# Moving the loads and stores of the normalised inputs, and the inputs of the output stage, from SyncE's DMA queue to those of ScalarE and GpSimd

## The chip, the cores and the metric

The kernel runs on one core of a Trainium2 chip. The time is the device time of one execution in microseconds, as the median of several runs; the profile is that of one further execution. Engines are called as in the profile: PE (TensorE), DVE (VectorE), ACT (ScalarE), POOL (GpSimd) and SP (SyncE). SP computes nothing here; it issues DMAs. ACT and POOL can issue DMAs too, each on a queue of its own and in the order of its own instructions.

## The reference

One layer over 8 sequences of 256 tokens with 512 features, all in float32:

```
xn = layernorm(x)
q, k, v = xn @ wq.T, xn @ wk.T, xn @ wv.T      # 32 query heads, 8 key and value heads, 128 wide
q, k = rotary(q), rotary(k)
scores = q k^T / sqrt(128), rescaled for some keys, causal
s = softmax(scores) v @ wo.T
gates = softmax over the two best of 4 experts of xn @ router_w.T
delta = sum over experts of gate * (xn @ A_e.T) @ B_e.T * 4
out = x + s * silu(delta)
```

## The kernel before

The 2048 tokens go through in four blocks (`tb`, 0 to 3) of two sequences (`b`, 0 and 1). For every block the kernel loops over the 8 groups of key heads (`g`). One step of a group makes the queries of the next group, computes scores and softmax for this one, multiplies the transposed probabilities with the values of the one before, and adds a part of the output projection. All large products use a scheme of seven block products in place of eight (the tiles `S1`, `S2`, `S4` and the operations `w`, `s`, `acc` that add tiles up). PSUM tiles that the profile names: `paq`, `peq`, `pdq` (queries), `pak`, `pek`, `pdk` (keys), `sc` (scores), `av` (values), `po` (output).

*Order.* No engine's order is written by hand. Every piece of work is a job in a `Plan`, given by `add(engine, takes, what, after, opens, closes, near, lag)`: the engine that it runs on, how long it occupies it, the jobs before it, the buffers that it takes and frees, a hint when it is due, and `lag`, the time from its end until its result can be used (a DMA's landing). The order of PE's jobs is laid by hand as due times. `Plan.run` plays the jobs through on the host with these costs and a hop of 0.18 us between engines; on each engine it starts the job that is due first among those that are ready. The instructions of an engine are issued in the order that comes out, and on the chip each waits for what it really depends on. All of them are recorded by a helper, so the profile gives line 118 for nearly everything.

*Normalised inputs.* `norm(tb)` loads the four row tiles `x` of a block, computes mean and deviation on DVE, and makes `xn`. The products need `xn` with features on partitions, the tile `XB`. For the first block PE transposes it. For the other three this is done with DVE and DMAs. DVE transposes 32x32 blocks (`turn_blocks`, profile name `x<-xn`); `spread(b)` stores the result to DRAM in four DMAs (`turned<-x`, 128 KB each); `gather(b)` reads it back in four DMAs (`XB<-turned`, 128 KB each, in pieces of 32 floats). DVE then adds up four tiles `XT` from both halves `b` of `XB`. There is one `XB` buffer (the room `X`), so a block's first gather waits until PE has read the last block's `XB` for the last time. In the plan, `gather(1)` also waits for the landing of `gather(0)`.

*Probabilities.* In `softmax(tb, g, b)`, ACT takes exponentials into `p`, DVE scales them and transposes 32x32 blocks into `blocks`. SP then stores these in four DMAs (`there<-blocks`) and, when they have landed, loads the transposed tile in one DMA of 768 KB (`pT<-there`), from which PE computes `av`. ACT copies `av` to `a`. There is one `p` and one `blocks` buffer.

*Output of a block.* `put_together(tb)` adds the seven accumulated products up. Its `inputs(b)` loads the gates (`g<-gates`) and rows of x (`xf<-in_x_dram`), 512 KB each, for the blocks 0 to 2; DVE multiplies and adds them, and SP stores the result. The last block has a function of its own, `last_products`.

*Queues.* Before the change SP issues the loads of `x`, both bounces (`turned`/`XB` and `there`/`pT`), the stores of the gates, `g` and `xf`, and the results. POOL issues the weight loads (`w`, `wo`, from rings of nine and eight tiles) and the stores of weight sums. ACT issues two table loads at the start and no other DMA.

Of the kernel before, what the change touches and what calls it, by code (L numbers as in the profile page):

```python
# [169 lines left out]
class Plan:  # L170
# [10 lines left out]
    def add(self, engine, takes, what, after=(), opens=(), closes=(), near=None, lag=0.0):  # L181
        after = [a for a in after if a]
        job = Job(engine, takes, what, after, opens, closes, near, lag, len(self.jobs))
        for a in after:
            a.then.append(job)
        for hold in closes:
            hold.readers += 1
        self.jobs.append(job)
        return job
# [71 lines left out]
def layer(ctx: ExitStack, tc: tile.TileContext, x, wquad, woquad, raT, bT, table, out):  # L261
    nc = InOrder(tc)
    pool = lambda name, bufs, **kw: ctx.enter_context(tc.tile_pool(name=name, bufs=bufs, **kw))
# [32 lines left out]
    add = plan.add  # L296
    rooms = {}

    def hold(tag):
        return Hold(rooms[tag])  # L300
# [9 lines left out]
    gates, sums_of, acts, weights, x_hold, loaded = {}, {}, {}, {}, {}, {}  # L310
# [7 lines left out]
    def norm(tb):  # L318
# [4 lines left out]
        xs, box = {}, {}  # L323
        xh = [hold("x") for _ in range(NB)]
# [42 lines left out]
        def new_acts():  # L367
            acts[tb] = (
                one.tile([P, NB, 2, 2, S], F32, tag="XB", name=f"XB{tb}"),
                one.tile([P, 4, 2, S], F32, tag="XT", name=f"XT{tb}"),  # L370
            )
# [6 lines left out]
        def turn_blocks(t):  # L378

            to = xs["x", t // 2].rearrange("p t d -> p (t d)")  # L380
            nc.vector.transpose(
                to.rearrange("p (q k t s) -> p t k q s", q=NQ, k=DC, t=2)[:, t % 2],
                box[t].rearrange("p (k q s) -> p k q s", q=NQ, s=BLK),
            )

        def spread(b):
            there = box["there", b] = turned.tile(
                [NQ, BLK, NQ, 2 * P], F32, tag=f"turned{b}", name=f"turned{tb}_{b}"
            )
            for a in range(NQ):  # L390
                nc.sync.dma_start(
                    out=there[:, :, a, :].rearrange("q r e -> r q e"),
                    in_=xs["x", b][bass.ts(a, BLK)]
                    .rearrange("r t d -> r (t d)").rearrange("r (q e) -> r q e", q=NQ),
                )

        def gather(b):
            if b == 0:
                new_acts()
            to = acts[tb][0][:, b].rearrange("p h c (t a s) -> p a (h c t) s", t=2, a=NQ)  # L400
            for a in range(NQ):
                nc.sync.dma_start(
                    out=to[:, a],
                    in_=box["there", b][:, :, a, :].rearrange("q r (k s) -> (q r) k s", s=BLK),
                )
# [10 lines left out]
        for t in range(NT):  # L416
            issues.append(
                add("sp", 0.45, lambda t=t: load(t), after=issues[-1:],
                    opens=[xh[t // 2]] if t % 2 == 0 else [])
# [3 lines left out]
                lag=8.5 if tb else (2.3, 2.6, 3.6, 4.0)[t])  # L423
# [6 lines left out]
        for ts in [slice(0, NT)] if tb else [slice(0, 2), slice(2, NT)]:  # L430
# [8 lines left out]
            for t in tiles:  # L439
                xn.append(  # L440
                    add("dve", 0.45, lambda t=t: normalise(t), after=[inv], opens=[mh[t]],
                        closes=[xh[t // 2]])
                )
        reads, pieces = [], []
        if tb:
            for b in range(NB):
                turns = [
                    add("dve", 0.6, lambda t=t: turn_blocks(t), after=xn[2 * b : 2 * b + 2], closes=[mh[t], xh[b]])
                    for t in (2 * b, 2 * b + 1)
                ]  # L450
                out_ = add("sp", 2.4, lambda b=b: spread(b), after=turns, closes=[xh[b]], lag=3.4)
                reads += [
                    add("sp", 2.4, lambda b=b: gather(b), after=[out_] + reads[:1],
                        opens=[] if b else [x_hold[tb]], lag=7.0)
                ] * 2
        for b, half in [] if tb else ((0, 0), (0, 1), (1, 0), (1, 1)):
            tp = add(
                "pe", 0.9, lambda b=b, h=half: turn(b, h), after=xn[2 * b : 2 * b + 2] + [identity],
                opens=[ph[2 * b + half]], closes=mh[2 * b : 2 * b + 2],
# [3 lines left out]
                    opens=[] if reads else [x_hold[tb]], closes=[ph[2 * b + half]], near=(tp, 0.5))  # L463
# [685 lines left out]
    def put_together(tb):  # L1149
        M = {k: acc[tb, k] for k in range(1, 8)}  # L1150

        def put(to, a, b, closes=()):
            near = max((M[a]["last"], M[b]["last"]), key=lambda p: p.number)
            M[to]["done"] = add(
                "dve", 0.61, lambda: nc.vector.tensor_add(M[to]["s"], M[a]["s"], M[b]["s"]),
                after=turn + [M[to]["done"], M[a]["done"], M[b]["done"]], closes=[M[k]["hold"] for k in closes],
                near=(near, 2.0),
            )
            M[to]["last"] = near

            turn[:] = [M[to]["done"]]

        loads, turn = {}, []

        def inputs(b):
            box = {}
            xh, gh = hold("x"), hold("x")
            rows = x[bass.ds(tb * TB + b * S, S), :].rearrange("(t p) o -> p t o", p=P)

            def load(what):  # L1170
                box[what] = x_pool.tile([P, 2, D], F32, tag="x", name=f"{what}{tb}_{b}")
                src = rows if what == "xf" else gates_dram[tb][:, bass.ts(b, 2), :]
                nc.sync.dma_start(out=box[what], in_=src)

            near = (M[2]["last"], -12.0)
            done = [
                add("sp", 0.3, lambda: load("g"), after=gates[tb][2 * b : 2 * b + 2], opens=[xh],
                    near=near, lag=9.0),
                add("sp", 0.3, lambda: load("xf"), opens=[gh], near=near, lag=9.0),
            ]  # L1180
            loads[b] = box, [xh, gh], done

        def result(k, b, f):
            box, holds, done = loads[b]
            s = lambda: M[k]["s"]
            cols = bass.ts(f, 2 * P)
            rows = out[bass.ds(tb * TB + b * S, S), cols].rearrange("(t p) o -> p t o", p=P)
            near = M[k]["last"]
            m = add(
                "dve", 0.61, lambda: nc.vector.scalar_tensor_tensor(  # L1190
                    s(), s(), 0.5, box["g"][:, :, cols], op0=ALU.mult, op1=ALU.mult
                ),
                after=[M[k]["done"], done[0]], closes=[holds[0]], near=(near, 3.0),
            )
            a = add(
                "dve", 0.61, lambda: nc.vector.tensor_add(s(), s(), box["xf"][:, :, cols]),
                after=[m, done[1]], closes=[holds[1]], near=(near, 4.0),
            )
            add(
                "sp", 0.3, lambda: nc.sync.dma_start(out=rows, in_=s()), after=[a],  # L1200
                closes=[M[k]["hold"]], near=(near, 5.0), lag=4.0,
            )

        inputs(0)
        put(2, 1, 2)
        result(2, 0, 0)
        put(1, 1, 6, [6])
        put(7, 1, 7)
        put(1, 1, 5)
        put(5, 7, 5)  # L1210
        put(4, 7, 4, [7])
        put(3, 1, 3, [1])
        result(3, 0, 1)
        inputs(1)
        result(5, 1, 1)
        result(4, 1, 0)
# [180 lines left out]


    tiles = norm(0)
    lead = []  # L1400
    for q in quads[0]:
# [5 lines left out]
    for n in range(len(steps) + 2):  # L1407
        last = n >= len(steps)
        tb, g = (NTB, 0) if last else steps[n]
# [6 lines left out]
        if not last:  # L1416
            if g == 1 and tb:
                route, turn, silus[tb] = experts(tb)
                fill += route
                later.append(turn)  # L1420
            at = g if tb == 0 else g - 2
            if 0 <= at < NT:
                fill += silus[tb][at]
            if tb + 1 < NTB and g == KV - 2:
                norm(tb + 1)
# [51 lines left out]
```

## Time and profile before

| | |
|---|---|
| median of 3 runs | 1347.17 us (1341.76 to 1347.25) |
| the profiled execution | 1345.25 us, its span 1343.5 us |
| busy: PE, DVE, ACT, POOL | 1325.6, 1102.8, 611.2, 314.3 us |
| mean granted TensorE clock | 0.999 |
| DMA | 282.10 MB, mean 210 GB/s |
| DMAs `turned<-x`, SP | 24, median 0.51 us to issue, 4.6 us to landing |
| DMAs `XB<-turned`, SP | 24, median 0.99 us to issue (0.38 to 4.54), 5.4 us to landing |
| DMAs `pT<-there`, SP | 64, median 0.34 us to issue (up to 3.73), 6.1 us to landing |
| DMAs `g<-gates` and `xf<-in_x_dram`, SP | 8 and 8, of which 6 and 6 in `inputs` |

How to read it: a row of the timeline has the start in us from the start of the span, the duration in us, the engine, the line, the operation and what it writes and reads; `x4` are four in a row, whose duration then reaches from the first start to the last end. In brackets stands how long the engine was idle before it, and for what. For a DMA on a queue the duration is the time that the issuing engine is occupied, not that of the transfer. A row of waits has the total, how often, and the longest.

### The profile page before, as it was taken

What the parts mean: (1) busy time and instruction counts of PE and PEld (TensorE: products, weight loads), DVE (VectorE), ACT (ScalarE), POOL (GpSimd) and SP (SyncE); (2) the same over time, 40 slices, a digit from 0 to 9 for tenths busy, and PEclk for the clock granted to TensorE, in tenths of its full rate; (3) what the DMA queues carried; (4) which work ended last, traced back from release to release, by engine and by line L of the source; (5) the groups of instructions that cost most, each with busy time, mean ns of one, the idle gap of its engine ahead of it and who ended that gap; (6) DMA issues with size and microseconds to landing.
All of it is one profiled execution on the core that took longest, in us unless ns stands there. A gap on an engine that the chain in (4) does not pass through costs nothing.

```text
span 1343.5 us, 19943 instructions
## 1 busy us (share of the span) xinstructions
PE 1325.6 (99%) x6488; PEld 1167.2 (87%) x6488; DVE 1102.8 (82%) x2835; ACT 611.2 (45%) x1576; POOL 314.3 (23%) x579
## 2 busy tenths in 40 slices
PE   9999999999999999999999999999999999999998
PEld 8888888888889888888888988888888898888886
DVE  6899989997978769788697875969868787686997
ACT  3474454543534435354353453535444454534531
POOL 2332232222222122221222212222122222222010
PEclk9999999999999999999999999999999999999999
DMA  6588677596766766768666676576876676666484
GB/s 212 165 264 253 203 217 226 197 261 205 244 178 199 223 202 185 232 210 221 205 223 202 214 208 216 175 236 210 227 221 191 220 219 205 191 189 199 137 282 135
DMA packets 134182, 282.10 MB, mean 210 GB/s; under 512 B 40832, under 2 KB 80896, under 8 KB 134080
## 3 DMA queue, kind: packets, MB, share of 16 engines
q0 software_dynamic: 45760, 149.98, 36.3%
q1 hardware_dynamic: 88096, 130.19, 31.7%
q8 instruction: 52, 0.85, 0.3%
q10 hardware_dynamic: 224, 0.66, 0.2%
q14 instruction: 50, 0.41, 0.1%
HBM read 197.94 MB, written 82.84 MB: 209 GB/s over the span
## 4 chain that ended last, share of the span: by engine, by line
PE 80%; DVE 10%; DMA 6%; SPq 2%; issue 1%; ACT 1%; DVEq 0%; ACTq 0%
PE po L118 21%; PE paq L118 15%; PE av L118 10%; PE sc L118 8%; PE pdq L118 7%; DMA pT<-there 5%; PE peq L118 4%; PE pak L118 4%; PE pav L118 4%; PE pdk L118 2%; SPq L118 2%; PE pdv L118 2%; DVE blocks L118 2%; DVE qTq L118 1%; DVE p L118 1%; DVE acc L118 1%
## 5 line engine op out<-in xcount | busy, mean ns | idle before, releaser
L118 ACT ACTIVATE p<-z,least 128x256 f32<-128x256 f32 (+7 forms) x512 | 207.6, 406 | 199.0 <-DVE least L118 130.3
L118 PE MATMUL po<-wo,a 128*128 128x256 f32 x992 | 233.0, 379 | 0.0
L118 PEld LDWEIGHTS po<-wo,a 128*128 128x128 f32 x992 | 186.7, 190 | 22.9
L118 PE MATMUL av<-pT,v 128*128 128x256 f32 x768 | 185.5, 380 | 8.2 <-DMA pT<-there 8.2
L118 PE MATMUL paq<-XT,w 128*128 128x256 f32 x768 | 182.0, 380 | 0.0
L118 DVE CUSTOM_DVE_ANT_0 z<-sc,tab 128x256 f32<-128x256 f32 (+7 forms) x512 | 134.1, 300 | 57.1 <-PE sc L118 54.1
L118 PE MATMUL po<-wo,s 128*128 128x256 f32 x744 | 177.6, 382 | 0.2 <-PE av L118 0.2
L118 PEld LDWEIGHTS av<-pT,v 128*128 128x128 f32 x768 | 145.0, 190 | 30.1 <-DMA pT<-there 6.1
L118 PEld LDWEIGHTS sc<-kk,qTq 128*128 128x128 f32 x1024 | 159.2, 191 | 12.6 <-DVE p L118 0.8
L118 PE MATMUL sc<-kk,qTq 128*128 128x256 f32 (+7 forms) x1024 | 168.0, 302 | 0.1
L118 PEld LDWEIGHTS paq<-XT,w 128*128 128x128 f32 x768 | 144.9, 190 | 19.5 <-ACT u2q L118 0.8
L118 POOL DMA_DIRECT2D w<-sums x144 | 79.2, 550 | 348.0 <-PE paq L118 143.9
L118 PEld LDWEIGHTS po<-wo,s 128*128 128x128 f32 x744 | 139.4, 190 | 23.4 <-issue 5.5
L118 ACT COPY a<-av 128x512 f32<-128x512 f32 x128 | 74.1, 580 | 180.8 <-PE av L118 180.6
L118 DVE TENSOR_TENSOR acc<-acc,po 128x512 f32<-128x512 f32 x189 | 127.7, 676 | 33.8 <-PE po L118 32.4
L118 ACT COPY swq<-cq 64x1024 f32<-64x1024 f32 x128 | 133.7, 1044 | 14.8 <-DVE cq L118 10.7
L118 POOL DMA_DIRECT2D w<-in_wquad_dram x148 | 80.9, 548 | 244.4 <-PE paq L118 84.6
L118 DVE STREAM_TRANSPOSE blocks<-p 128x1024 f32<-128x1024 f32 (+1 forms) x128 | 123.7, 968 | 0.4 <-DMA there<-blocks 0.2
L118 DVE TENSOR_SCALAR p<-p,total 128x256 f32<-128x256 f32 (+7 forms) x512 | 117.2, 294 | 2.3
L118 DVE TENSOR_TENSOR qTq<-cq,tab 128x1024 f32<-128x1024 f32 x64 | 77.9, 1218 | 26.2 <-ACT cq L118 26.0
L118 ACT ACTIVATION_READ_ACCUMULATOR p<-z,least 128x1 f32 x512 | 95.8, 187 | 0.0
L118 POOL DMA_DIRECT2D wo<-in_woquad_dram x104 | 56.9, 548 | 132.5 <-PE po L118 122.3
(137 smaller groups left out, 1853.3 us busy)
## 6 DMA issues: line engine op xcount, KB each, us to landing
there<-blocks SPq DMA_DIRECT2D x256, 192.0 KB, 3.8
pT<-there SPq DMA_DIRECT2D x64, 768.0 KB, 6.1
w<-in_wquad_dram POOLq DMA_DIRECT2D x148, 256.0 KB, 4.7
w<-sums POOLq DMA_DIRECT2D x144, 256.0 KB, 4.1
wo<-in_woquad_dram POOLq DMA_DIRECT2D x104, 256.0 KB, 5.0
wo<-osums POOLq DMA_DIRECT2D x96, 256.0 KB, 4.7
sums<-w POOLq DMA_DIRECT2D x48, 256.0 KB, 4.4
osums<-wo POOLq DMA_DIRECT2D x32, 256.0 KB, 4.7
```

The lines of the kernel that those rows point to most:

```text
L118: ins = what(*args, **kwargs)
```

## The change

Three groups of DMAs change their queue, and the plan's costs for them are changed with it.

- `spread` (24 DMAs): from SP to POOL. The job is charged to POOL with 2.4 us as before, and its lag goes from 3.4 to 8.0.
- `gather` (24 DMAs): from SP to ACT. The job is charged to ACT with 0.4 us in place of SP's 2.4; its lag stays 7.0.
- the loads in `inputs` (12 DMAs): from SP to POOL, charged with 0.8 us in place of 0.3.

The loads `x<-in_x_dram`, the bounce of the probabilities, the stores of gates and results, and the loads in `last_products` stay on SP.

```diff
             for a in range(NQ):
-                nc.sync.dma_start(
+                nc.gpsimd.dma_start(
                     out=there[:, :, a, :].rearrange("q r e -> r q e"),
...
             for a in range(NQ):
-                nc.sync.dma_start(
+                nc.scalar.dma_start(
                     out=to[:, a],
                     in_=box["there", b][:, :, a, :].rearrange("q r (k s) -> (q r) k s", s=BLK),
                 )
...
-                out_ = add("sp", 2.4, lambda b=b: spread(b), after=turns, closes=[xh[b]], lag=3.4)
+                out_ = add("pool", 2.4, lambda b=b: spread(b), after=turns, closes=[xh[b]], lag=8.0)
                 reads += [
-                    add("sp", 2.4, lambda b=b: gather(b), after=[out_] + reads[:1],
+                    add("act", 0.4, lambda b=b: gather(b), after=[out_] + reads[:1],
                         opens=[] if b else [x_hold[tb]], lag=7.0)
                 ] * 2
...
                 src = rows if what == "xf" else gates_dram[tb][:, bass.ts(b, 2), :]
-                nc.sync.dma_start(out=box[what], in_=src)
+                nc.gpsimd.dma_start(out=box[what], in_=src)
...
-                add("sp", 0.3, lambda: load("g"), after=gates[tb][2 * b : 2 * b + 2], opens=[xh],
+                add("pool", 0.8, lambda: load("g"), after=gates[tb][2 * b : 2 * b + 2], opens=[xh],
                     near=near, lag=9.0),
-                add("sp", 0.3, lambda: load("xf"), opens=[gh], near=near, lag=9.0),
+                add("pool", 0.8, lambda: load("xf"), opens=[gh], near=near, lag=9.0),
```

## The prediction

> **What bounds the kernel now.** I read the page's busy times first, then the waits of PE, then the waiting rows in PE's timeline with SP's, ACT's and DVE's rows beside them.
>
> ```profile
> PE 1325.6 (99%) x6488; PEld 1167.2 (87%) x6488; DVE 1102.8 (82%) x2835; ACT 611.2 (45%) x1576; POOL 314.3 (23%) x579
> ...
> q1 hardware_dynamic: 88096, 130.19, 31.7%
> q10 hardware_dynamic: 224, 0.66, 0.2%
> ...
> PE av L118 <- DMA pT<-there: 8.2, 7, 1.8
> ```
>
> PE is busy 1325.6 of 1343.5 us. Of the 17.9 us left, 8.2 are waits of the value products `av` for the transposed probabilities `pT`, in seven places; no other wait of PE in this list is over 1.4 us. So a change of queues can win at most 8.2 us, and only by bringing `pT` earlier. The change touches SP's queue at the three changes of token block, near 284, 617 and 948 us. PE's timeline has four of the seven waits there:
>
> ```profile
> 289.29 1.56 PE L118 MATMUL av<-pT,v 128*128 128x256 f32 x6 [1.33 <-DMA pT<-there]
> 309.07 1.56 PE L118 MATMUL av<-pT,v 128*128 128x256 f32 x6 [0.90 <-DMA pT<-there]
> 641.63 1.56 PE L118 MATMUL av<-pT,v 128*128 128x256 f32 x6 [1.49 <-DMA pT<-there]
> 971.46 1.56 PE L118 MATMUL av<-pT,v 128*128 128x256 f32 x6 [0.81 <-DMA pT<-there]
> ```
>
> They sum to 1.33 + 0.90 + 1.49 + 0.81 = 4.53 us, 0.34% of the time. The other 3.7 us are near 100, 383 and 1305 us, where none of the moved transfers runs. Second, SP's queue at the middle change (columns: start, duration):
>
> ```profile
> 617.44 3.88 SPq L118 DMA_DIRECT2D XB<-turned  x4
> 625.82 2.25 SPq L118 DMA_DIRECT2D there<-blocks  x4
> 628.11 4.24 SPq L118 DMA_DIRECT2D XB<-turned  x4
> 632.52 3.22 SPq L118 DMA_DIRECT2D pT<-there  x1
> ```
>
> The issue of `pT` at 632.52 takes 3.22 us where it takes 0.34 elsewhere, behind four loads of `XB` that themselves hold SP 4.24 us. This is what the change removes. Third, what ACT and DVE do at that moment:
>
> ```profile
> 618.34 0.38 ACT L118 ACTIVATE p<-z,least 128x96 f32<-128x96 f32 x1 [1.57 <-DVE least L118]
> ...
> 622.87 0.58 ACT L118 COPY a<-av 128x512 f32<-128x512 f32 x1 [3.43 <-PE av L118]
> ...
> 620.21 0.20 DVE L118 RECIPROCAL total<-total 128x8 f32<-128x8 f32 x1
> ...
> 628.71 0.69 DVE L118 TENSOR_TENSOR s<-a,a 128x512 f32<-128x512 f32 x1
> ```
>
> The last exponentials of the unit whose `pT` is late at 641.6 run on ACT at 618.34, inside the 3.88 us in which SP issues the first `XB` load. DVE waits for them with its reciprocal, and DVE is full there (13.71 of 15.00 us busy between 617 and 632).
>
> **The change part by part.**
>
> *Stores of the normalised inputs to GpSimd* (24 DMAs, `turned<-x`). They leave SP 24 x 0.51 = 12 us (median row) and add to POOL 24 x 0.55 = 13 us (0.546 us, the weight loads of 128 partitions). It matters on SP once: at 273 us eight of them hold it 6.4 us, and `pT` is issued at 279.66. There the 1.33 us should go. On POOL they stand between weight loads, wait for DVE's transposes (`x<-xn`), and weight loads are queued behind them. What hides that: the weights come nine tiles deep, and PE has no wait for a weight load in the whole list. Without that cover it would be 4 x 0.55 = 2.2 us a group. Their landing (4.6 us from SP; POOL's 256 KB loads take 4.1 to 5.0) is hidden by the wait for the last read of `XB`: SP waited 14.9 us in all for PE's `pdq`. I take zero.
>
> *Gates and x for the output to GpSimd* (12 DMAs, 0.4 to 1.0 us each on SP; on POOL 0.55 to 1.1). SP issues them after `pT` (338.18 after 337.80; 426.92 after 426.53), so their leaving frees nothing that is waited for. On POOL they could be held behind a weight load; DVE's waits for `xf` and `g` sum to 3.3 us now. I take zero, from -1 to +2.
>
> *Loads of `XB` to ScalarE* (24 DMAs in six groups of four). On SP the groups took 8.01 and 5.29, 3.88 and 4.24, 4.91 and 3.75 us: 30.1 in all. The gain on SP: `pT` can be issued about 6.5 us after its stores begin (265.50 - 259.08 = 6.4; 643.69 - 637.17 = 6.5), so at 617 it gains 632.52 - 632.3 = 0.2 and 3.22 - 0.34 = 2.9, together 3.1 us; at 284 it gains 300.92 - 299.6 = 1.3 and 1.03 - 0.34 = 0.7, together 2.0.
>
> The cost on ACT is not shown in this trace, and two rows bound it. ACT issued two DMAs at the start, `tab` in 0.38 us and `bt` in 0.53: a group of four would hold ACT 1.8 us. Against this, the Trainium skill (Perfetto Trace Analysis, section "DMA Instruction — HWDGE (DVE, Sync)") says that the issuing sequencer is held until all descriptors of a transfer have been generated. By that a transfer keeps its issue time on any such queue, SP's 3.75 to 8.01 us a group. With 1.8 us the exponentials are hardly late and the sum of the whole change is -4.5; with SP's times it is the positive sum below. I take SP's rows, because they are the same transfer: queue 10 carried 224 packets of some 3 KB, while the window around 284 us has 2506 of 3657 packets under 512 B.
>
> What that does, with the first group of each change of block. It begins when PE has read `XB` for the last time (617.4). The exponentials of 618.34 have 0.9 us of room, their followers on DVE 0.7 (they end at 619.43, the reciprocal starts at 620.21), and SP's relief gives 3.1: a hold up to 4.7 us is repaid. At 284 the room is 1.3 + 0.8 + 2.0 = 4.1. Holds of 3.88 and 4.91 give -0.8 and +0.2 at the second and third change. At the first, a hold of 4.4 (mean of those two) gives +0.3 and one of 8.01 gives +3.9, less the 1.33 won by the stores. The three sum to -1.6 at the least and +2.0 at the most; I take +0.2.
>
> The second group adds to it. In the plan the loads of one group wait for the landing of the other; with 0.4 us on ACT and a lag of 7.0 the second is put 0.4 + 7.0 + 0.18 = 7.6 us behind the first, near 625.0 (before 2.4 + 7.0 + 0.18 = 9.6). With 4 us it holds ACT to 629, past the copy `a<-av` of 626.80. That copy is then 3 us late, the sums `s<-a,a` (628.71) and the next begin about 1.8 late, and PE's products with `s` at 631.44, which have 0.8 us of room, start some 0.9 late. Three times 0.9 is +2.7. For the same reason PE's first key product is laid 2 us earlier in the plan than `XB` has landed so far (from the first issue, on SP, 7 to 9 us at 617): a wait of 0 to 1.2 us, on the same stretch of PE as the 0.9, so not added.
>
> Sum: 0 + 0 + 0.2 + 2.7 = **+3 us**. The profiled execution took 1345.25 us (span 1343.5 and 1.75 around it), which gives 1348.2; the median of the runs shown is 1.9 above it, so I state 1347.2 + 3 = **1350**.
>
> **The rivals.**
>
> *The relief is all that is seen.* ACT is only 45% busy, and its queue was otherwise empty of DMAs, so a group may pass in under 2 us, as `tab` and `bt` did. Then all 4.53 us go and nothing comes: 1342.6. Against it: 1024 pieces of 128 B a group don't become fewer on another queue.
>
> *ACT's queue becomes the bound at the three changes (slower).* One mechanism: ACT stands at the `XB` loads as long as SP did at 284 us, 8 us, and DVE and then PE wait for exponentials and copies. It decides from a hold of 4.7 us. At 8 us the second group makes `a<-av` 7 instead of 3 us late, and PE's loss of 0.9 becomes 4.9; three times is +15: 1362. For it: the planner charges 0.4 us for the group, so it puts nothing else there. Against it: the 8 us arose while `pT` and the stores shared SP's queue.
>
> *Little changes but the order.* The planner's new costs re-lay the neighbouring instructions; PE has almost nothing to win by that (17.9 us idle, half of it at start and end), and a few us to lose. It widens the first case rather than being one.
>
> **How the numbers follow.** About 0.5%, 6.7 us, is what a measurement of this kernel can tell from no change. The forecast (+3, from -1 to +8) gets 0.45: 0.37 within 0.5%, 0.08 slower. The relief gets 0.22: 0.18 within, and 0.04 faster, since 4.53 us is not enough for it alone. The slower rival gets 0.33: 0.31 slower, 0.02 within. Faster 0.04, same 0.57, slower 0.39. The range is from the relief, 1342.5, to just over the slower rival, 1363.
>
> **What would show it.** Right: DMA issues `XB<-turned` on ACT's queue of about 1 us each, some 4 us a group; the reciprocal after them later by 2 to 3 us; issues of `pT` back at 0.34 us near 301, 632 and 962; PE's waits for `pT` near 289 gone, and new short waits of PE for `s`, `XB` or ACT's copies. Wrong: `XB` issues of 0.4 us on ACT and no wait of PE at the three changes (the relief), or waits of 3 us and more there with DVE idle for ACT (the slower rival), or long waits of PE for `w`, which would break the cover that I gave POOL.

## Result and the profile after

The changed kernel takes 1351.49 us (median of 11 runs) against 1342.65 us for the kernel before on the same chip. The ratio is 1.0056, 95% interval 1.0043 to 1.0069: slower by some 7.5 us, a little over the 0.5% that the prediction took as the least that can be told from no change. The profiled execution took 1349.37 us, 4.1 us more than the profiled execution before; its span is 1347.4 us.

The page's busy times and queues, the waits of PE, and the rows of the moved DMAs (in those: duration at least, median and at most in ns, then the first and last start in us):

```profile
PE 1326.3 (98%) x6488; PEld 1167.6 (87%) x6488; DVE 1104.6 (82%) x2835; ACT 610.9 (45%) x1576; POOL 332.3 (25%) x615
...
q10 hardware_dynamic: 25184, 3.81, 1.7%
```

```profile
PE sc L118 <- DVE least L118: 3.9, 3, 1.8
...
PE av L118 <- DMA pT<-there: 1.9, 2, 1.5
```

```profile
L118 POOL DMA_DIRECT2D turned<-x x24: 553/565/781, 272.7 to 942.8; - x24
L118 ACTq DMA_DIRECT2D XB<-turned x24: 366/974/3243, 283.8 to 958.5; - x24
```

PE does the same work (1326.3 us; 1325.6 before). The 25,000 small packets of the `XB` loads are now on queue 10. The waits for `pT` fell from 8.2 to 1.9 us: the 4.53 us at the three changes are gone, and the wait near 110 us (1.53 us before) now stands in the list as one of 1.64 us for ACT's `p`. In their place stand 3.9 us for the scores `sc`, which were not in the list before. A load of `XB` holds ACT 0.97 us at the median, as it held SP (0.99).

All rows of PE's timeline at the three changes of block in which PE waited over 0.6 us:

```profile
295.13 0.85 PE L118 MATMUL sc<-kk,qTq 128*128 128x96 f32 x6 [1.26 <-DVE least L118]
...
297.34 1.97 PE L118 MATMUL pak<-XB,w 128*128 128x256 f32 x8 [1.35 <-DMA wo<-in_woquad_dram]
...
301.67 1.97 PE L118 MATMUL po<-wo,s 128*128 128x256 f32 x8 [0.63 <-DVE s L118]
...
307.65 1.97 PE L118 MATMUL pdk<-XT,w 128*128 128x256 f32 x8 [0.66 <-PE sc L118]
...
630.86 0.85 PE L118 MATMUL sc<-kk,qTq 128*128 128x96 f32 x6 [1.76 <-DVE least L118]
...
640.95 1.97 PE L118 MATMUL pdk<-XT,w 128*128 128x256 f32 x8 [0.62 <-PE sc L118]
...
961.72 0.85 PE L118 MATMUL sc<-kk,qTq 128*128 128x96 f32 x6 [0.89 <-DVE least L118]
...
971.82 1.97 PE L118 MATMUL pdk<-XT,w 128*128 128x256 f32 x8 [0.63 <-PE sc L118]
```

They sum to 7.80 us where the four waits for `pT` summed to 4.53: +3.3 of the 3.9 us by which the span grew. Two releasers must not be taken at their word. `pak` reads `XB` and `w`, not `wo`; the last load of the group was issued at 287.67 and took 9.5 us to land, which is 297.2, so the wait is for `XB`; a load of `w` issued beside it took 6.7 us. `pdk` reads `XT`, which DVE adds up from `XB`. This wait is for DVE, not for `XB`: at the middle change the last loads were issued from 626.44 and took 3.6 us to land, but the first sum `XT` starts at 640.19, with no idle time before it, behind other work of DVE, and `pdk` starts 0.1 us after its end. DVE's timeline:

```profile
639.03 1.25 DVE L118 STREAM_TRANSPOSE blocks<-p 128x1024 f32<-128x1024 f32 x1
640.19 0.66 DVE L118 TENSOR_TENSOR XT<-XB 128x512 f32<-128x512 f32 x1
```

The middle change shows how a load becomes a wait for scores. ACT's timeline, then DVE's, then SP's:

```profile
619.06 5.58 ACTq L118 DMA_DIRECT2D XB<-turned  x4
624.69 0.38 ACT L118 ACTIVATE p<-z,least 128x96 f32<-128x96 f32 x1 [6.30 <-DMA XB<-turned]
...
626.44 2.14 ACTq L118 DMA_DIRECT2D XB<-turned  x3
```

```profile
625.83 0.20 DVE L118 RECIPROCAL total<-total 128x8 f32<-128x8 f32 x1 [3.92 <-ACT p L118]
...
630.08 0.39 DVE L118 CUSTOM_DVE_ANT_0 z<-sc,tab 128x256 f32<-128x256 f32 x1
```

```profile
631.45 2.24 SPq L118 DMA_DIRECT2D there<-blocks  x4
...
636.74 0.34 SPq L118 DMA_DIRECT2D pT<-there  x1
```

The first group holds ACT 5.58 us, and the last exponentials of the unit wait 6.30 us for their turn. DVE then waits 3.92 us with the reciprocal, and what is queued behind it comes late by as much. The first `z` of the next unit starts 4.25 us after the reciprocal, as it did before (reciprocal at 620.21, and this row of DVE's timeline before):

```profile
624.46 0.39 DVE L118 CUSTOM_DVE_ANT_0 z<-sc,tab 128x256 f32<-128x256 f32 x1
```

PE's next scores wait for a reduction `least` behind that `z`, and start at 630.86. That the `z` operations free their place in PSUM is read from this order, not shown. The issue of `pT` is back at 0.34 us, and from the start of the stores `there` to the end of that issue pass 5.6 us in place of 9.9. But the stores start 5.6 us later than before, so this `pT` lands near 643.7 (7.0 us after its issue), where before it landed at 641.6. PE does not wait for it because PE is late itself and has `pdk` and `pak` in front of `av`, which starts at 644.48.

The timed runs lost more than the profiled one. The mean granted clock was 0.9968 in the runs of the changed kernel and 0.9985 in 51 runs of the kernel before (those taken beside the first experiments below). If the time goes with the clock, 0.0017 of 1350 us is an estimated 2.3 us. The profiled execution had a clock of 1.000, so those 2.3 us come on top of its 4.1. The remaining 1.1 us are not explained.

### The profile page after: what moved, and what is told of

It reads as the page before. It is cut to its first block, busy times and chain, and to the rows that moved or that the text cites. A ratio compares the mean times of both kernels' runs of the same rounds, so it can differ in the third digit from the quotient of the medians.

```text
span 1347.4 us, 19990 instructions
## 1 busy us (share of the span) xinstructions
PE 1326.3 (98%) x6488; PEld 1167.6 (87%) x6488; DVE 1104.6 (82%) x2835; ACT 610.9 (45%) x1576; POOL 332.3 (25%) x615
## 4 chain that ended last, share of the span: by engine, by line
PE 80%; DVE 12%; DMA 4%; issue 2%; ACT 1%; ACTq 1%; SPq 0%; DVEq 0%; POOL 0%; POOLq 0%
PE po L118 22%; PE paq L118 14%; PE av L118 10%; PE sc L118 8%; PE pdq L118 7%; PE pak L118 4%; PE pav L118 4%; PE peq L118 4%; PE pdk L118 2%; PE pdv L118 2%; DVE blocks L118 2%; DVE p L118 2%; DVE acc L118 2%; DVE qTq L118 1%; DVE z L118 1%
```

## Which part of the change costs: two halves

**Only the `XB` loads on ACT.** Everything else stays on SP. The plan has the change's costs for the loads.

```diff
-                nc.sync.dma_start(
+                nc.scalar.dma_start(
                     out=to[:, a],
...
-                    add("sp", 2.4, lambda b=b: gather(b), after=[out_] + reads[:1],
+                    add("act", 0.4, lambda b=b: gather(b), after=[out_] + reads[:1],
```

> Only the loads of XB move to ACT's queue, with the plan's costs of the change; stores and output inputs stay on SP. Theory (ACT is held while it issues the XB loads, its exponentials come late, DVE stops for them and PE waits for DVE): nearly the whole loss is here, 1.003 to 1.007 of the time before, ACT held 4 to 9 us at each of the six groups. Rival one (the queue of POOL: stores, gates and x delay weights or the output): 0.998 to 1.001. Rival two (only the plan's new costs re-lay the order badly): the same as the theory, since this kernel has those costs.

Measured: 1.0065 (1.004 to 1.009), span 1348.2 us. The waits are in part others than in the change: PE waits 2.79 us for `sc` at the three changes, and also 1.71 and 2.09 us for `pT` near 608 and 940, which the change does not have.

**Only the stores, the gates and x on POOL.** The `XB` loads stay on SP. The plan has the change's costs for what moves.

```diff
-                nc.sync.dma_start(
+                nc.gpsimd.dma_start(
                     out=there[:, :, a, :].rearrange("q r e -> r q e"),
...
-                nc.sync.dma_start(out=box[what], in_=src)
+                nc.gpsimd.dma_start(out=box[what], in_=src)
...
```

> Only the stores of the normalised inputs and the inputs of the output stage move, to POOL; the XB loads stay on SP with the costs before. Theory (ACT's hold): no loss, 0.997 to 1.001; the wait of PE for pT near 289 us (1.33 us) goes, those near 309, 642 and 971 us stay, as SP still issues the XB loads. Rival one (POOL's queue): most of the loss, 1.003 to 1.007, with PE or DVE waiting for w, g or xf. Rival two (plan's costs): little, 0.998 to 1.002.

Measured: 1.0000 (0.9987 to 1.0013), span 1343.6 us. In PE's timeline the waits for `pT` near 289 and 309 are gone; the other two remain:

```profile
641.34 1.56 PE L118 MATMUL av<-pT,v 128*128 128x256 f32 x6 [1.12 <-DMA pT<-there]
...
972.15 1.56 PE L118 MATMUL av<-pT,v 128*128 128x256 f32 x6 [0.80 <-DMA pT<-there]
```

What follows: the whole loss lies in the `XB` loads on ACT, with the costs that the plan gave them. The POOL part removes 1.33 + 0.90 us of waits at the first change, gets a new wait of 0.81 us of `pak` there, and has no effect on the median that can be told.

## Why the loads on ACT cost: the order that was planned round them

**The plan is told the true hold.** The kernel is the changed one, but `gather` is charged with 4.6 us, near what a group takes (3.24 to 8.86 us, 5.2 in the mean), and the lag is 4.6. So the plan has `XB` landed 9.2 us after the start of a group, where the change had 7.4 and the kernel before 9.4.

```diff
-                    add("act", 0.4, lambda b=b: gather(b), after=[out_] + reads[:1],
-                        opens=[] if b else [x_hold[tb]], lag=7.0)
+                    add("act", 4.6, lambda b=b: gather(b), after=[out_] + reads[:1],
+                        opens=[] if b else [x_hold[tb]], lag=4.6)
```

> The whole change, but the plan charges ACT 4.6 us for a group of XB loads and takes a lag of 4.6 (9.4 us from start to landing with the hop, about what was measured on SP) in place of 0.4 and 7.0. Theory (ACT's hold): the hold remains, so the exponentials behind it are as late; PE's wait for XB goes; 1.002 to 1.006. Rival two (the plan knew nothing of the hold, and a true cost repairs the order): 0.998 to 1.001. Rival one (POOL's queue): as slow as the change, 1.004 to 1.007.

Measured: 0.9993 (0.9983 to 1.0003), span 1342.4 us: the whole loss is gone, as the rival said and not as the theory did. The hold is not (8.30 us at 284.44, and 5.3 us from 618.17). ACT's timeline, then DVE's:

```profile
623.51 0.37 ACT L118 ACTIVATE p<-z,least 128x96 f32<-128x96 f32 x1 [6.02 <-DMA XB<-turned]
```

```profile
620.93 0.68 DVE L118 TENSOR_TENSOR acc<-acc,po 128x512 f32<-128x512 f32 x1
...
622.30 0.69 DVE L118 TENSOR_TENSOR acc<-acc,po 128x512 f32<-128x512 f32 x1 [0.68 <-PE po L118]
...
624.65 0.20 DVE L118 RECIPROCAL total<-total 128x8 f32<-128x8 f32 x1 [1.66 <-ACT p L118]
...
625.64 0.42 DVE L118 CUSTOM_DVE_ANT_0 z<-sc,tab 128x256 f32<-128x256 f32 x1
```

The exponentials wait 6.02 us, as in the change. But DVE does sums `acc` meanwhile, so that the reciprocal waits 1.66 us in place of 3.92, and the next unit's `z` follows 1.0 us after it in place of 4.25. PE has no wait at the second and third change; at the first, 1.23 us for `sc` and 1.33 for `s` are left. So the changed kernel loses by the wrong costs in its plan: 0.4 us was written where a group takes some 5, and DVE's work was lined up behind a reciprocal that could not start. The edit corrects two things at once, the hold and the landing of `XB`, and no run parts them. In the change's trace the waits for `sc` go back to the hold; the early `pak` and `pdk` fit a landing that was planned too early, but this is argued.

**Each load a job of its own.** A group is four jobs of 1.15 us on ACT, so that the plan may put exponentials and copies between them; `XB` counts as landed 4.6 us after the last.

```diff
-        def gather(b):
-            if b == 0:
+        def gather(b, a):
+            if b == a == 0:
...
-            for a in range(NQ):
-                nc.scalar.dma_start(
+            nc.scalar.dma_start(
...
+                part = []
+                for a in range(NQ):
+                    part.append(
+                        add("act", 1.15, lambda b=b, a=a: gather(b, a),
+                            after=[out_] + reads[:1] + part[-1:],
+                            opens=[] if b or a else [x_hold[tb]])
+                    )
+                reads += [add("dma", 0.0, lambda: None, after=part, lag=4.6)] * 2
```

> The whole change, but each of the four XB loads of a group is a job of its own on ACT, charged 1.15 us, with XB usable 4.6 us after the last; the planner may put exponentials and copies between the loads and knows the whole hold. Theory (a hold of ACT that the plan does not know is what costs): better than before, 0.996 to 0.999, with SP's relief kept and DVE's reciprocals waiting under 2 us. Rival (any hold of ACT costs, known or not): 1.000 to 1.004.

Measured: 1339.62 us (median of 5 runs), 0.9968 (0.9956 to 0.9980), span 1338.3 us. It has the lowest ratio of this study and is faster than both the kernel before and the change. ACT's timeline, one row of DVE's, and the row of the loads:

```profile
613.55 0.37 ACTq L118 DMA_DIRECT2D XB<-turned  x1
614.44 0.38 ACT L118 ACTIVATE p<-z,least 128x96 f32<-128x96 f32 x1 [1.57 <-DVE least L118]
614.76 0.37 ACTq L118 DMA_DIRECT2D XB<-turned  x1
615.22 0.75 ACTq L118 DMA_DIRECT2D XB<-turned  x1
616.06 2.35 ACTq L118 DMA_DIRECT2D XB<-turned  x1
...
618.97 0.58 ACT L118 COPY a<-av 128x512 f32<-128x512 f32 x1 [3.42 <-PE av L118]
```

```profile
616.31 0.20 DVE L118 RECIPROCAL total<-total 128x8 f32<-128x8 f32 x1
```

```profile
L118 ACTq DMA_DIRECT2D XB<-turned x24: 366/367/3300, 283.1 to 957.2; - x24
```

The exponentials pass after the first load and wait for DVE alone, the reciprocal waits for nothing, and three loads lie in the gap before `a<-av`. PE has no wait at any of the three changes.

The division does more than tell the plan. A load that stands apart from the others holds ACT 0.37 us only, now the median, and all loads together hold it about 20 us in place of 31. So this kernel has a hold that is known, divided and shorter; which of the three brings it below the 0.9993 of the one charged job is not parted.

**The same division on SP.** The kernel before, with its loads as four jobs of 1.15 us, on SP's queue. The stores, gates and x are on SP too.

```diff
...
-                    add("sp", 2.4, lambda b=b: gather(b), after=[out_] + reads[:1],
-                        opens=[] if b else [x_hold[tb]], lag=7.0)
...
+                        add("sp", 1.15, lambda b=b, a=a: gather(b, a),
```

> The kernel before, all queues as they were (SP issues stores, XB loads, gates and x), with one edit: the four XB loads of a group are jobs of their own on SP, charged 1.15 us each, with XB usable 4.6 us after the last. It tells whether e5_four_jobs wins by the move of the queue or by the division into jobs with true costs alone. If by the move: 0.999 to 1.001 here, with PE's waits for pT at the three changes of block left. If by the division: 0.996 to 0.998.

Measured: 1.0015 (1.0004 to 1.0026). Its profiled execution, 5 us above its median, lists these waits of PE:

```profile
PE av L118 <- DMA pT<-there: 7.0, 5, 2.3
...
PE pak L118 <- ACT a L118: 4.0, 3, 1.5
```

The waits for `pT` that were expected to stay are at the first change only (2.08 and 1.52 us); near 642 and 971 they are gone, and `pak` waits 1.48 and 1.46 us for ACT's `a` in the re-laid order. So the division gains nothing by itself. With these pieces the gain needs both: the queues of the change, and a plan that knows the hold. Four jobs on SP with the stores on POOL were not run.

## Whether the hold itself must be there

**Pieces of 1 KB in place of 128 B.** Same bytes, queues and plan as in the change; the features come in a wrong order.

```diff
-            to = acts[tb][0][:, b].rearrange("p h c (t a s) -> p a (h c t) s", t=2, a=NQ)
+            to = acts[tb][0][:, b].rearrange("p h c s -> p (h c s)").rearrange("p (a e) -> p a e", a=NQ)
...
-                    in_=box["there", b][:, :, a, :].rearrange("q r (k s) -> (q r) k s", s=BLK),
+                    in_=box["there", b][:, :, a, :].rearrange("q r e -> (q r) e"),
```

> The whole change with its plan, but the XB loads write each partition's 1 KB as one piece in place of eight of 128 B (the features then lie in another order than the products assume; bytes, waits and plan are those of the change). Theory (ACT is held by the number of pieces): a group of four holds ACT 1.5 to 2.5 us, under the 4.7 that the relief of SP repays; the loss goes, 0.996 to 1.000, and PE's waits for pT at the three changes of block are gone. Rival one (POOL's queue) and rival two (the plan's order): still 1.004 to 1.007, since both are unchanged.

**Pieces of 256 B.** The same, with half as many pieces as in the change.

```diff
...
-                    in_=box["there", b][:, :, a, :].rearrange("q r (k s) -> (q r) k s", s=BLK),
+                    in_=box["there", b][:, :, a, :].rearrange("q r (k s) -> (q r) k s", s=2 * BLK),
```

> As the change, but the XB loads write pieces of 256 B in place of 128 B (half as many; features in another order than the products assume; bytes and plan are those of the change). It doses the hold between the change (1.0056) and the kernel with 1 KB pieces (0.9973). Prediction's break-even of 4.7 us: a hold of 2 to 3 us a group is repaid by SP's relief, so 0.997 to 1.001. If instead any hold over the 0.4 us that the plan charges is passed on to PE: half of the way from 0.9973 to 1.0056 or more, 1.0015 to 1.004.

Measured: 0.9973 (0.9962 to 0.9984) with 1 KB, 0.9995 (0.9983 to 1.0007) with 256 B. Rows of the loads, of the first and then of the second:

```profile
L118 ACTq DMA_DIRECT2D XB<-turned x24: 326/389/1065, 284.0 to 952.2; - x24
```

```profile
L118 ACTq DMA_DIRECT2D XB<-turned x24: 366/465/3528, 283.7 to 953.6; - x24
```

The median hold of a load is 0.39, 0.47 and 0.97 us for 128, 512 and 1024 pieces. With 128 a group holds ACT 1.8 to 2.6 us, so the plan's 0.4 us is still too low, but the loss turns into a gain with queue and plan unchanged. With 512 one group still holds ACT 6.12 us. So a shorter hold is enough to cure the loss, and so is a plan with true costs. The number of pieces does not set the hold alone: four separate jobs with 1024 pieces each have a median of 0.37 us. In these traces it is the loads close behind one another that take longer.

**Long reads for short stores.** The stores write the bounce buffer in the order of `XB`, 16 DMAs a group in pieces of 128 B on POOL, charged with 9.0 us; one DMA in pieces of 4 KB reads it.

```diff
-                [NQ, BLK, NQ, 2 * P], F32, tag=f"turned{b}", name=f"turned{tb}_{b}"
+                [NQ, BLK, 8, NQ, BLK], F32, tag=f"turned{b}", name=f"turned{tb}_{b}"
...
+                in_=box["there", b].rearrange("q r k a s -> (q r) (k a s)"),
```

> The small pieces are moved from the loads to the stores: the bounce buffer in DRAM lies in the order of XB, the stores write pieces of 128 B in 16 DMAs of 256 pieces on POOL (charged 9 us in the plan), and XB is read back in one DMA of 4 KB pieces on ACT. Theory (the number of pieces holds the issuing engine): ACT is held under 1 us a group, and the loss turns into the gain of the long pieces, 0.996 to 0.999, if POOL's 16 issues a group stay hidden behind the deep weight rings. Rival (POOL is the tight queue): PE waits for w or wo, or the stores land late and ACT stands waiting for them, 1.003 to 1.010.

Measured: 1.0018 (1.0008 to 1.0028), span 1343.2 us. The moved DMAs, then PE's worst row at the first change, then DVE's row before it:

```profile
L118 POOL DMA_DIRECT2D turned<-x x96: 553/756/1247, 263.0 to 928.8; - x96
L118 ACTq DMA_DIRECT2D XB<-turned x6: 326/326/337, 285.7 to 954.6; - x6
```

```profile
307.39 2.78 PE L118 MATMUL pdk<-XT,w 128*128 128x256 f32 x8 [2.44 <-issue]
```

```profile
305.47 1.25 DVE L118 STREAM_TRANSPOSE blocks<-p 128x1024 f32<-128x1024 f32 x1 [2.48 <-DMA there<-blocks]
```

ACT is held 0.33 us in place of some 5, and yet it is no win: one wait of 2.44 us, and then eight matmuls in 2.78 us in place of 1.97. DVE stands 2.48 us before a transpose into `blocks`, whose last stores take 8.4 us to land (median on the page before: 3.8). The sum `XT` follows at 306.64, and `pdk` reads it. Why the stores land late is not shown; on POOL nine other DMAs leave between 284.9 and 289.9, behind the 16 stores. The timed runs had a mean clock of 0.9972 against 0.9987, an estimated 2.0 us of the 2.4 lost.

**The loads on POOL.** The change with `gather` on POOL, charged with its hold, as one job:

```diff
-                nc.scalar.dma_start(
+                nc.gpsimd.dma_start(
...
+                    add("pool", 4.6, lambda b=b: gather(b), after=[out_] + reads[:1],
+                        opens=[] if b else [x_hold[tb]], lag=4.6)
```

> The whole change, but the XB loads go to POOL too, charged 4.6 us with a lag of 4.6, so ACT issues none. It measures what 1024 pieces a DMA-group cost POOL. Theory (ACT's hold was the loss): if POOL issues a group in about 5 us, the loss is gone, 0.996 to 1.000. If POOL needs much longer for many pieces than for 128 (0.55 us a DMA), XB and the weights behind it come late and PE waits for XB, w or wo: 1.003 to 1.015.

And as four jobs of 0.9 us, with `gather(b, a)` (the lines are compared with the four jobs on ACT):

```diff
-                        add("act", 1.15, lambda b=b, a=a: gather(b, a),
+                        add("pool", 0.9, lambda b=b, a=a: gather(b, a),
```

> The four loads of a group as jobs of their own, as in e5_four_jobs, but on POOL and charged 0.9 us (what POOL took for one in e8_loads_pool). No hold of ACT at all. If a known, divided hold of ACT costs nothing any more, this is as fast as e5_four_jobs: 0.996 to 0.998. If what is left of ACT's hold still costs, it is faster: 0.993 to 0.996. If POOL's order delays weights: 0.999 to 1.003.

Measured: 0.9984 (0.9971 to 0.9997) as one job, 0.9986 (0.9976 to 0.9997) as four. The loads of the first of the two:

```profile
L118 POOL DMA_DIRECT2D XB<-turned x24: 884/892/910, 284.7 to 952.6; - x24
```

POOL takes a steady 0.89 us for a load that took ACT 0.37 to 3.24. Both kernels are a little faster than the one before; neither beats the four jobs on ACT (their intervals touch or overlap, so by little at most). Here the division makes no difference that can be told. The second falls between its expectations.

## First group or second

The prediction put +0.2 us on the first groups and +2.7 on the second. Two kernels move only one of the two, with the plan's 0.4 us; the other group stays on SP with 2.4.

```diff
-                nc.scalar.dma_start(
+                (nc.scalar if b == 0 else nc.sync).dma_start(
...
+                    add("act" if b == 0 else "sp", 0.4 if b == 0 else 2.4, lambda b=b: gather(b), after=[out_] + reads[:1],
```

> As the change, but only the first group of XB loads of each change of block (sequence 0) is on ACT with 0.4 us; the second stays on SP with 2.4. The prediction's sum put +0.2 us on the first groups and +2.7 on the second. By that: 0.998 to 1.001. By what the trace of the change shows (DVE's reciprocal waits 2.9 to 3.9 us for the exponentials behind the first group, and PE then for DVE's reductions): most of the loss, 1.002 to 1.005.

The other kernel has `b == 1` in both places.

> The other half: only the second group (sequence 1) of each change of block is on ACT with 0.4 us, the first stays on SP with 2.4. By the prediction's sum (copies of av late, then the sums s, then PE's products with s): most of the loss, 1.001 to 1.004. By the trace of the change: little or a gain, 0.997 to 1.000, since SP no longer issues loads in front of pT.

Measured: first group alone 1.0100 (1.008 to 1.012), second alone 1.0046 (1.0025 to 1.0066). The first is slower than either of its expectations, the second just above the higher of its two. They don't add up to the change's 1.0056, and they are not clean halves. With the first alone, the two groups run at the same time on two queues. ACT's and SP's timelines and the DMAs (KB each, us to landing):

```profile
283.27 5.92 ACTq L118 DMA_DIRECT2D XB<-turned  x4
```

```profile
284.17 10.30 SPq L118 DMA_DIRECT2D XB<-turned  x4
```

```profile
XB<-turned ACTq DMA_DIRECT2D x4, 128.0 KB, 8.9
XB<-turned SPq DMA_DIRECT2D x4, 128.0 KB, 12.1
```

SP is held 10.30 us and the loads land after 12.1 us; before, the group at this place held SP 8.01 us and landed after 8.4. The mean clock of the timed runs was 0.9935 against 0.9983, an estimated 6.5 us of the 14.6 lost. With the second alone, the order differs again, and PE waits for `XB` itself (its timeline):

```profile
296.61 3.11 PE L118 MATMUL pak<-XB,w 128*128 128x256 f32 x8 [3.08 <-DMA XB<-turned]
```

How the loss divides between the groups stays open: whichever group moves, the other one's transfer changes with it.

## Why the prediction was right, and where it was not

- *The hold on ACT.* Right. The prediction took SP's rows over those of `tab` and `bt`, and the six groups hold ACT 5.08, 8.86, 5.58, 3.66, 4.71 and 3.24 us, 31.1 in all (30.1 on SP). This agrees with what the Trainium skill says (Perfetto Trace Analysis, section "DMA Instruction — HWDGE (DVE, Sync)"), that the issuing sequencer is free again only after all descriptors have been made; 1.8 us a group does not agree.
- *SP's relief, 4.53 us.* Right on SP: the issues of `pT` take 0.34 us again, and all four waits are gone. But the near cause is not SP alone: at the second and third change `pT` lands some 2 and 3 us later than before, and PE, late and in another order, comes to `av` later still. The kernel with four jobs is the one that wins about this much.
- *Stores and output loads on POOL, 0.* Right. A store takes POOL 0.565 us (0.55 was taken), the one wait that PE's list puts down to `wo` is one for `XB`, and the kernel with this part alone measures 1.0000.
- *First groups, +0.2.* The net is near (3.91 us of waits for `sc` less the 4.53 us of waits that went is -0.6), the path is not, so that the number came out by luck. The step that failed followed the late exponentials only to `pT`, where they would be repaid by the relief. It left out the next unit's `z`, queued on DVE behind the waiting reciprocal, which PE needs sooner than `pT`.
- *Second groups, +2.7 by `a<-av` and `s`.* The path is mostly wrong: `s` shows once, 0.63 us. PE waits 1.35 us for `XB` (0 to 1.2 was given and not added) and 1.91 for `pdk` (0.66, 0.62 and 0.63), whose `XT` stands behind other work of DVE; that wait the prediction did not have. With 0.63 that is 3.89.
- *The sum, +3.* The trace has -0.6 + 3.9 = +3.3 at the three changes, by terms that partly stood in for others. The ratio stands for 7.5 us; the 2.3 of them that the clock is estimated to make were in no step. That 1350 lies so near to the measured 1351.49 is luck too: it started from 1347.2, the median of three runs, where the median of eleven is 1342.65, so the start was 4.5 us too high and the change 4.5 us too small.
- *The relief as rival.* Not what the change does, but what it could do: with the plan told the hold in four jobs, the ratio 0.9968 is 4.3 us less than before, close to the 4.53.
- *ACT as the bound.* A group did hold ACT 8.86 us at the first change, and no PE wait of 4.9 us followed: the largest of the three after it is 1.35. So the step from hold to loss was too steep; why so little came through was not followed.
- *Two readings.* The other three waits for `pT` lie near 110, 393 and 1313 us, not 100, 383 and 1305. And 1024 pieces of 128 B are one load, not a group of four (24,960 more packets on queue 10 for 24 loads). Neither bears on the sum.

## What to carry to other kernels

A DMA issue occupies the engine that issues it, here for 0.37 to 3.24 us. Read from the queue's row in the profile how long, and charge that, and the landing, in any schedule before moving the issue to a compute engine; the loss here came from the costs in the plan (0.4 us for a hold of some 5), not from the move. When an engine is late, follow not only its own consumer but everything queued behind the waiting instruction on the next engine. Divide a run of long issues so that urgent work can pass between them; here the issues themselves became shorter by it.

## What was not expected of the hardware

After a wait of PE of some 2 us or more, the granted clock can fall, and a good part of the wait is paid again. In the kernel with the first group alone, PE's row and two windows (length; busy us of PE, weight loads, DVE, ACT and POOL with counts; granted clock; DMA share; GB/s):

```profile
299.67 3.75 PE L118 MATMUL pak<-XB,w 128*128 128x256 f32 x8 [3.41 <-DMA there<-blocks]
```

```profile
296.00:300.00 4.00, 0.59 (x4) 0.51 (x4) 3.93 (x18) 3.77 (x17) 0.00 (x0) 0.77 0.99 179
300.00:304.00 4.00, 4.00 (x10) 3.17 (x10) 1.52 (x5) 0.54 (x1) 0.28 (x1) 0.50 0.58 147
```

Eight matmuls take 3.75 us in place of 1.97, at a clock of 0.50. The same shows in other kernels after shorter waits, here the POOL part alone, long reads for short stores, and four jobs on SP:

```profile
111.18 4.37 PE L118 MATMUL av<-pT,v 128*128 128x256 f32 x12 [2.43 <-DMA pT<-there]
```

```profile
109.73 4.51 PE L118 MATMUL av<-pT,v 128*128 128x256 f32 x12 [1.89 <-DMA pT<-there]
```

```profile
291.02 2.90 PE L118 MATMUL av<-pT,v 128*128 128x256 f32 x6 [2.08 <-DMA pT<-there]
```

Twelve such matmuls take 2.83 us at full clock, six 1.56. The granted clock was 0.79 between 108 and 116 us in the first two, and 0.51 between 291 and 294 in the third. But the length alone does not decide: with the `XB` loads alone on ACT, twelve after a wait of 2.09 us at 940.45 took 2.86 us, and with the first group alone, six after 2.75 us at 399.08 took 1.53. What else it needs is open. It can make a schedule with several waits of 2 us worse than their sum, and is a likely, not a shown, reason for the lower clock in the timed runs of the changed kernel.
